# The opening of a block kernel rearranged: first input half ahead of the columns, statistics ahead of the SiLU, late zero products out, W_B's first block ahead of its shift

## The chip, the cores and the metric

The kernel runs on one core of a Trainium2 chip. The metric is device time in microseconds (us) of one execution, and the figure compared is the median over runs. A core has five instruction streams that matter here: TensorE (PE in the profile, with its weight loads as PEld), VectorE (DVE), ScalarE (ACT), GpSimd (POOL) and SyncE (SP), which in this kernel issues all the DMAs. Each engine runs its own stream strictly in order and waits on semaphores that other engines or DMAs raise.

## The reference

The input `x` has 16 sequences of 1024 positions and 256 features, all in float32. What is computed, cut to what matters:

```python
mod = (silu(c) @ wmod).reshape(16, 6, 1, -1)       # c: 16 x 256
sa, ca, ga, sb, cb, gb = (mod[:, n] for n in range(6))
ga, gb = [sign(g) * max(abs(g), 0.25) for g in (ga, gb)]
h = layernorm(x) * (1 + ca) + sa
Bu = (h @ W_B.T + b_B) * dt                        # dt = exp(log_dt)
xs[t] = A_bar * xs[t - 1] + Bu[t]                  # A_bar = exp(-exp(log_A) * dt)
x = x + ga * (xs @ W_C.T + b_C + h @ W_D.T + b_D)
h = layernorm(x) * (1 + cb) + sb
y = square(relu(h @ W_fc.T)) @ W_proj.T            # 256 -> 1024 -> 256
x = x + gb * (spikes in five steps driven by y) / 5
```

Three things in it are needed at the very start: the modulation (`silu(c)` times parts of `wmod`), the decay `A_bar`, and the statistics of the first rows of `x`.

## The kernel before

The work is cut into 32 tiles of 512 positions. A tile has two halves of work. Half "a": statistics, normalised rows `xn_a`, turned so that features lie on partitions, scaled to `h_a`, products with W_B (`pb`), a scan along positions (`xs`), products with W_D and W_C that add up in `py`, and the residual sum `x1`. Half "b": statistics of `x1`, `h_b`, the products `pf` with W_fc and `pp` with W_proj, and the spike count. Each matrix product is done in three passes on float32 operands split into a rounded high part and a remainder ("hi" and "lo"): hi by hi, weight lo by data hi, weight hi by data lo. With two blocks of 128 on the contraction that makes six TensorE products for each 128 x 512 result. The order of passes is `PASSES = ((0, 0), (1, 0), (0, 1))`, with the weight's part first (line 228).

All engine calls go through a small class that keeps each engine's instructions in the order in which the program is written (lines 71 to 83), so nothing is moved by a scheduler. Because that helper records every instruction, nearly all rows of the profile carry the same line, L81, and one goes by the names of the tiles instead.

The change touches only the opening, from the first loads to the turned rows of tile 1; the later periods, two tiles or so deep in a software pipeline, are as before. In the order in which TensorE meets it, the opening of the kernel before is:

- Loads on SP's queue (lines 125 to 152): the columns `col` (20.5 KB with c, the log of A, the biases and the log of dt), the first tile's rows `xq` in two halves of 256 KB, then parts of `wmod` (`wm1`), W_B (`fb`), W_D (`fd`), W_C (`fcm`), the second tile's rows, and more.
- `run_idle(12)` (line 612): twelve products of a tile of zeros into `ps_zero`, whose result is not used. `run_idle(3)` follows twice more (lines 616, 618).
- `silu_c` (line 182): three exponentials on ScalarE from `col`, then three VectorE steps that make `sil` = silu(c).
- `columns` (line 212) multiplies `sil` with a part of `wmod`: `ps_ca`, `ps_sa`, `ps_ga`, `ps_cb`, `ps_sb`, four small products each, which the profile shows as eight.
- `decay(n)` (line 208) issues the next n of 20 tiny VectorE steps that make `abar` (a polynomial, then squared eight times); they are strewn between other VectorE work.
- `moments`, `aggregate`, `root`, `newton_v` (lines 250 to 310): the statistics (`st_a`, `mv_a`), a square root on ScalarE (`q_a`), and five VectorE steps to the scale `r_a` and the offset `m_a`. `normalise_by` (line 324) then makes `xn_a`, four blocks of 128 x 256, each on the engine that a list names: V for VectorE, S for ScalarE.
- `transpose` turns `xn_a` into `pt_a` on TensorE; `scaled_hi` (ScalarE) and `scaled_lo` (VectorE) make `h_a`; `wb`, `wd` and `wc` are the split weights, hi on ScalarE and lo on VectorE.
- `ps_bb`, the shift `sa` times W_B, gives `bias_b`; `state_input` is `pb`; `state_bias` and `state_scan` give `bu` and `xs`; `mix_h` and `mix_xs` are `py`; `ps_ga` and `ps_bd` give the gate `ga` and its offset `gac` (`shift_gate`, line 658).
- `mix_out_late` makes `x1` (tile `x` in the profile) on ScalarE and VectorE, and `transpose_back` turns it into `pm`, from which tile 0's half "b" starts.

Of the kernel before, what the change touches and what calls it, by code (L numbers as in the profile page):

```python
# [21 lines left out]
F32 = mybir.dt.float32  # L22
# [7 lines left out]
KD = D // P  # L30
# [56 lines left out]
def adaln_kernel(ctx: ExitStack, tc: tile.TileContext, x, xq, w_bT, w_cT, w_dT, w_fcT, w_projT, cols,  # L87
# [35 lines left out]
        Q.dma_start(out=xqs[t], in_=xq[t])  # L123

    col = const.tile([P, KD * NB + 4 * KD + 1], F32, name="col")
    Q.dma_start(out=col, in_=cols)
    xqs[0] = io.tile([P, SUB, D], F32, tag="xq", name="xq_0", bufs=2)
    for s in (slice(0, 2), slice(2, 4)):
        Q.dma_start(out=xqs[0][:, s], in_=xq[0][:, s])
    cs = col[:, 0:KD * NB].rearrange("p (k b) -> p k b", k=KD)  # L130
    la, bb, bc, bd = (col[:, KD * (NB + n):KD * (NB + n + 1)] for n in range(4))
    ldt = col[:, KD * (NB + 4):]
# [49 lines left out]
    def silu_c():  # L182

        S.activation(sil, cs, AF.Exp, scale=-1.0)
        S.activation(edt, ldt, AF.Exp)
        S.activation(ea, la, AF.Exp)
        V.tensor_scalar(sil, sil, 1.0, None, ALU.add)
        V.reciprocal(sil, sil)
        V.tensor_tensor(sil, sil, cs, ALU.mult)

    def decay_steps():


        yield V.tensor_scalar(z, ea, edt, -1.0, ALU.mult, ALU.mult)
        yield V.tensor_scalar(z, z, -104.0, 1.0 / 256, ALU.max, ALU.mult)
        factor, r = 1.0, z
        for n in range(9, 1, -1):
            factor *= n
            yield V.scalar_tensor_tensor(abar, r, factor, z, ALU.add, ALU.mult)
            r = abar  # L200
        yield V.tensor_scalar(abar, abar, 1.0 / factor, None, ALU.mult)
        for _ in range(8):
            yield V.scalar_tensor_tensor(abar, abar, 2.0, abar, ALU.add, ALU.mult)
        yield V.tensor_scalar(abar, abar, 1.0, None, ALU.add)
# [3 lines left out]
    def decay(n):  # L208
        for _ in range(n):
            next(steps, None)  # L210

    def columns(wm, which, name):

        ps = ps_f.tile([P, KD, NB], F32, tag="ps_f", name=f"ps_{name}")
        for m in range(KD):
            at = which * D + m * P
            for k in range(KD):
                PE.matmul(ps[:, m], lhsT=wm[:, k, at:at + P], rhs=sil[:, k], start=k == 0, stop=k == KD - 1)
        return ps
# [27 lines left out]
    def blocks_of(x):  # L247
        return lambda s: x[:, s]

    def moments(key, src, between=lambda: None, blocks=range(SUB)):  # L250
        if key not in norms:
            n = norms[key] = Norm()
            n.sts = [small.tile([P, 6], F32, tag=f"st{s}{key[0]}", name=f"st_{key}_{s}", bufs=2)
                     for s in range(SUB)]
        for s in blocks:
            V.bn_stats(norms[key].sts[s], src(s))
            between()
# [14 lines left out]
    def root(key):  # L272
        n = norms[key]
        n.q = small.tile([P, SUB], F32, tag="q", name=f"q_{key}")
        if hasattr(n, "v"):
            S.activation(n.q, n.v, AF.Sqrt)
        else:
            S.activation(n.q, n.mv[:, :, 1], AF.Sqrt, bias=eps)
# [19 lines left out]
    def newton_v(key, between=lambda: None):  # L298

        n = norms[key]  # L300
        n.e, n.r, n.m = (small.tile([P, SUB], F32, tag=tag, name=f"{tag}_{key}") for tag in "erm")
        V.reciprocal(n.q, n.q)
        between()
        V.scalar_tensor_tensor(n.e, n.q, -0.5, n.q, ALU.mult, ALU.mult)
        between()
        V.scalar_tensor_tensor(n.e, n.mv[:, :, 1], EPS, n.e, ALU.add, ALU.mult)
        between()
        V.scalar_tensor_tensor(n.r, n.e, 1.5, n.q, ALU.add, ALU.mult)
        between()
        V.scalar_tensor_tensor(n.m, n.mv[:, :, 0], -1.0, n.r, ALU.mult, ALU.mult)  # L310
# [13 lines left out]
    def normalise_by(key, src, engines):  # L324

        n = norms.pop(key)
        xn = work.tile([P, SUB, D], F32, tag="xn", name=f"xn_{key}", bufs=3)
        for s, E in enumerate(engines):
            if E is S:
                S.activation(xn[:, s], src(s), AF.Identity, bias=n.m[:, s:s + 1], scale=n.r[:, s:s + 1])  # L330
            else:
                E.tensor_scalar(xn[:, s], src(s), n.r[:, s:s + 1], n.m[:, s:s + 1], ALU.mult, ALU.add)
        xns[key] = xn
# [37 lines left out]
        for k in range(KD):  # L371
            S.activation(hs[key][:, 0, k], src(k), AF.Identity, scale=scale[:, k])

    def scaled_lo(key, src):
        h, scale = hs[key], scale_of(key)
        for k in range(KD):
            V.scalar_tensor_tensor(h[:, 1, k], src(k), scale[:, k], h[:, 0, k].bitcast(F32),
                                   ALU.mult, ALU.subtract)

    def turned_hi(key):  # L380
        scaled_hi(key, lambda k: vs[key][:, k])
# [7 lines left out]
    def transpose(key, pool=ps_f, tag="ps_f"):  # L389

        xn = xns.pop(key)
        for k in range(KD):
            ps = pts[key, k] = pool.tile([P, TT], F32, tag=tag, name=f"pt_{key}_{k}")
            for s in range(SUB):
                dst = ps[:, s * P:(s + 1) * P]
                if key[0] == "a":
                    dst = ps.rearrange("p (q s u) -> p s q u", s=SUB, u=32)[:, s]
                PE.transpose(dst, xn[:, s, k * P:(k + 1) * P], ident)
# [11 lines left out]

    pbs = {}

    def state_input(t):
        h = hs[f"a{t}"]
        for m in range(KD):
            ps = pbs[t, m] = ps_f.tile([P, TT], F32, tag="ps_f", name=f"pb_{t}_{m}")
            products(ps, lambda i, k: wb[:, i, k, m * P:(m + 1) * P], lambda j, k: h[:, j, k], True, True, True)

# [21 lines left out]
    def state_lo(t, blocks=slice(0, KD)):  # L440
        V.tensor_tensor(xsps[t][:, 1, blocks], xss[t][:, blocks], xsps[t][:, 0, blocks].bitcast(F32),
                        ALU.subtract)

    def mix_part(t, w, v, first, last):
        for passes in (PASSES[:2], PASSES[2:]):
            for m in range(KD):
                products(ys[t, m], lambda i, k: w[:, i, k, m * P:(m + 1) * P], lambda j, k: v[:, j, k],
                         first and passes[0] == PASSES[0], last and passes[0] != PASSES[0], True, passes, True)

    def mix_h(t):  # L450
        for m in range(KD):
            ys[t, m] = ps_y.tile([P, TT], F32, tag="ps_y", name=f"py_{t}_{m}")
        mix_part(t, wd, hs[f"a{t}"], True, False)

    def mix_xs(t):
        mix_part(t, wc, xsps[t], False, True)
# [151 lines left out]
    def run_idle(n):  # L608
        for _ in range(n):
            PE.matmul(ps_zero, lhsT=zero[:, 0:P].bitcast(F32R), rhs=zero.bitcast(F32R), start=True, stop=True)  # L610

    run_idle(12)
    silu_c()
    S.activation(sa[:, 0, 0:1], edt, AF.Sqrt)
    ps_ca = columns(wm1, 1, "ca")
    run_idle(3)
    ps_sa = columns(wm1, 0, "sa")
    run_idle(3)
    decay(3)
    moments("a0", blocks_of(xqs[0]), between=lambda: decay(1))  # L620
    aggregate("a0")
    root("a0")
    S.activation(wb[:, 0], fb, AF.Identity, scale=edt)
    newton_v("a0", lambda: decay(1))
    normalise_by("a0", blocks_of(xqs[0]), (V, S, V, S))
    S.activation(sa, ps_sa, AF.Copy)
    V.tensor_scalar(s1, ps_ca, 1.0, None, ALU.add)
    V.scalar_tensor_tensor(wb[:, 1], fb, edt, wb[:, 0].bitcast(F32), ALU.mult, ALU.subtract)
    transpose("a0")
    decay(5)  # L630

    ps_bb = ps_p.tile([P, KD, NB], F32, tag="ps_p", name="ps_bb")
    for m in range(KD):
        for k in range(KD):
            PE.matmul(ps_bb[:, m], lhsT=fb[:, k, m * P:(m + 1) * P], rhs=sa[:, k],
                      start=k == 0, stop=k == KD - 1)
    scaled_hi("a0", lambda k: pts["a0", k])
    scaled_lo("a0", lambda k: pts["a0", k])
    S.activation(wd[:, 0], fd, AF.Copy)
    for m in range(KD):  # L640
        V.tensor_scalar(bias_b[:, m], ps_bb[:, m], bb[:, m:m + 1], edt, ALU.add, ALU.mult)
    decay(8)
    V.tensor_tensor(wd[:, 1], fd, wd[:, 0].bitcast(F32), ALU.subtract)
    S.activation(wc[:, 0], fcm, AF.Copy)
    state_input(0)
    state_bias(0)
    state_scan(0, (0,))
    moments("a1", blocks_of(xqs[1]), blocks=(0, 1))
    mix_h(0)

    ps_ga = columns(wm1, 2, "ga")
    ps_bd = ps_p.tile([P, KD, NB], F32, tag="ps_p", name="ps_bd")
# [13 lines left out]

    state_hi(0, slice(0, 1))
    state_scan(0, (1,))
    moments("a1", blocks_of(xqs[1]), blocks=(2, 3))
    aggregate("a1")  # L670
    root("a1")
    state_hi(0, slice(1, 2))
    V.tensor_tensor(wc[:, 1], fcm, wc[:, 0].bitcast(F32), ALU.subtract)
    state_lo(0, slice(0, 1))
    gates = shift_gate()
    newton_v("a1", lambda: next(gates, None))
    state_lo(0, slice(1, 2))
    for _ in gates:
        pass
    normalise_by("a1", blocks_of(xqs[1]), (S, S, V, S))  # L680
    mix_xs(0)
    transpose("a1")
    ps_cb = columns(wm2, 1, "cb")
    ps_sb = columns(wm2, 0, "sb")
    mix_out_late(0)
    V.tensor_scalar(s2, ps_cb, 1.0, None, ALU.add)
    scaled_hi("a1", lambda k: pts["a1", k])
# [349 lines left out]
```

## Time and profile before

| | us |
|---|---|
| median of 3 runs | 992.76 (991.89 to 993.47) |
| the profiled execution | 991.63 |
| its span, first to last instruction | 989.8 |
| TensorE busy (PE) | 981.9, 99% of the span |
| VectorE busy (DVE) | 851.1, 86% |
| ScalarE busy (ACT) | 767.1, 77% |
| GpSimd busy (POOL) | 284.5, 29% |
| granted TensorE clock, mean over the span | 0.999 |

Times in the views are counted from the span's start. A row gives start, duration, engine, operation, tiles as out<-in, how often, and in brackets how long the engine had been idle and who ended that. Ends of matrix products are modelled by the profiler, so TensorE's busy time includes short waits between products; where waits of a tenth of a microsecond matter, distances between starts are used.

### The profile page before, as it was taken

How to read it: one execution, taken by the hardware profiler on the slowest of the kernel's cores; microseconds unless marked ns; L12 is line 12 of the kernel's file. 1: busy time of each engine (PE TensorE's matmuls, PEld its weight loads, DVE VectorE, ACT ScalarE, POOL GpSimd, SP SyncE). 2: the span in 40 equal slices, each digit the busy share in tenths (PEclk: the TensorE clock that was granted, in tenths of full speed). 3: DMA queues.
4: the chain of work that ended last, by engine and by line, in shares of the span. 5: the costliest groups of instructions: out<-in, count | busy, mean ns of one | idle time of the engine just before them, and what ended most of it. 6: DMA issues, size and time to landing. Idle time of an engine off the chain costs nothing.

```text
span 989.8 us, 13366 instructions
## 1 busy us (share of the span) xinstructions
PE 981.9 (99%) x4410; PEld 813.8 (82%) x4410; DVE 851.1 (86%) x1618; ACT 767.1 (77%) x1142; POOL 284.5 (29%) x313
## 2 busy tenths in 40 slices
PE   9999999999999999999999999999999999999997
PEld 8888788888888888888888888888888888888886
DVE  8789998888988889888889888889888889887777
ACT  6786887787877887877877877877877878777784
POOL 0002243223233223233133333133332233331122
PEclk9999999999999999999999999999999999999999
DMA  8224555455454455554455454554554554443321
GB/s 312 83 82 153 179 182 149 149 171 168 153 170 137 152 179 153 157 171 133 154 179 158 155 172 127 169 170 152 168 152 146 170 167 153 149 139 128 96 86 43
DMA packets 125350, 150.07 MB, mean 152 GB/s; under 512 B 9568, under 2 KB 89184, under 8 KB 125280
## 3 DMA queue, kind: packets, MB, share of 16 engines
q1 hardware_dynamic: 125280, 149.22, 48.1%
q8 instruction: 34, 0.56, 0.2%
q14 instruction: 36, 0.29, 0.1%
HBM read 85.22 MB, written 63.96 MB: 151 GB/s over the span
## 4 chain that ended last, share of the span: by engine, by line
PE 91%; DVE 5%; ACT 2%; issue 1%; DMA 0%; SPq 0%; DVEq 0%
PE pf L81 33%; PE pp L81 32%; PE py L81 16%; PE pb L81 8%; DVE o L81 2%; PE ps_zero L81 1%; ACT a L81 1%; ACT xn_a L81 1%; ACT hid L81 0%; DMA hop_x<-w_x 0%; DVE h_b L81 0%; DVE st_b L81 0%; DVE x L81 0%; DVE h_a L81 0%; DVE e_b L81 0%
## 5 line engine op out<-in xcount | busy, mean ns | idle before, releaser
L81 PE MATMUL pp<-hid,wp 128*128 128x512 f32 (+1 forms) x1560 | 365.4, 387 | 0.4 <-DVE o L81 0.4
L81 PE MATMUL pf<-h_b,wf 128*128 128x512 f32 x1536 | 363.9, 390 | 0.0
L81 PEld LDWEIGHTS pp<-hid,wp 128*128 128x128 f32 x1560 | 289.2, 188 | 61.4 <-DVE hid L81 1.5
L81 PEld LDWEIGHTS pf<-h_b,wf 128*128 128x128 f32 x1536 | 288.1, 188 | 59.8
L81 ACT ACTIVATE a<-pf,bias_f 128x512 f32<-128x512 f32 x256 | 167.0, 680 | 157.1 <-PE pf L81 157.0
L81 DVE TENSOR_TENSOR hid<-a,hid 128x1024 fp32r<-128x1024 f32 x127 | 152.8, 1223 | 89.2 <-ACT hid L81 89.2
L81 POOL TENSOR_TENSOR o<-o,x 128x512 f32<-128x512 f32 x64 | 110.0, 1739 | 296.0 <-ACT o L81 296.0
L81 DVE SCALAR_TENSOR_TENSOR o<-pp,o 128x512 f32<-128x512 f32 (+1 forms) x260 | 177.5, 683 | 8.0
L81 ACT ACTIVATE hid<-a 128x1024 fp32r<-128x1024 f32 x128 | 135.9, 1061 | 4.0
L81 ACT ACTIVATE a<-a 128x1024 f32<-128x1024 f32 x128 | 135.8, 1061 | 3.9
L81 POOL TENSOR_SCALAR x<-x,gac 128x512 f32<-128x512 f32 x58 | 90.2, 1564 | 51.8 <-DVE o L81 51.8
L81 POOL TENSOR_SCALAR v_a<-mv_a 128x4 f32<-128x4 f32 x26 | 15.6, 600 | 278.0 <-DVE mv_a L81 278.0
L81 PE MATMUL py<-xsp,wc 128*128 128x512 f32 x384 | 92.7, 390 | 0.0
L81 PE MATMUL pb<-h_a,wb 128*128 128x512 f32 x384 | 92.6, 390 | 0.0
L81 PE MATMUL py<-h_a,wd 128*128 128x512 f32 x384 | 92.2, 389 | 0.0
L81 PEld LDWEIGHTS py<-h_a,wd 128*128 128x128 f32 x384 | 72.1, 188 | 14.9
L81 PEld LDWEIGHTS pb<-h_a,wb 128*128 128x128 f32 x384 | 71.9, 188 | 15.0
L81 PEld LDWEIGHTS py<-xsp,wc 128*128 128x128 f32 x384 | 71.8, 188 | 15.0 <-DVE xsp L81 0.3
L81 ACT ACTIVATE xn_a<-xq,m_a,r_a 128x256 f32<-128x256 f32 x123 | 63.8, 592 | 3.2 <-DVE m_a L81 3.2
L81 ACT ACTIVATE xn_b<-xm,m_b,r_b 128x256 f32<-128x256 f32 x120 | 62.0, 588 | 4.0 <-DVE m_b L81 4.0
L81 DVE TENSOR_SCALAR o<-pp 128x512 f32<-128x512 f32 (+1 forms) x65 | 43.4, 668 | 14.1 <-PE pp L81 14.1
L81 ACT ACTIVATE o<-o,gb 128x512 f32<-128x512 f32 x64 | 42.3, 709 | 6.2 <-issue 4.7
(124 smaller groups left out, 835.6 us busy)
## 6 DMA issues: line engine op xcount, KB each, us to landing
x<-in_x SPq DMA_DIRECT2D x32, 512.0 KB, 5.1
out<-o SPq DMA_DIRECT2D x63, 256.0 KB, 6.9
xq<-in_xq SPq DMA_DIRECT2D x31, 512.0 KB, 6.7
hop_a<-w_a SPq DMA_DIRECT2D x120, 128.0 KB, 2.2
v_a<-hop_a SPq DMA_DIRECT2D x30, 512.0 KB, 4.0
hop_x<-w_x SPq DMA_DIRECT2D x120, 128.0 KB, 3.1
xm<-hop_x SPq DMA_DIRECT2D x30, 512.0 KB, 3.2
hop_b<-w_b SPq DMA_DIRECT2D x120, 128.0 KB, 2.2
```

The costliest lines, as they stand in the source:

```text
L81: return self.tc.keep_in_program_order(issue(*args, **kwargs))
```

## The change

In words:

- Loads: the first half of tile 0's rows is issued ahead of `col`, which now stands between the two halves.
- `silu_c` keeps its three exponentials; its three VectorE steps become the first three steps that `decay` hands out. The statistics of tile 0 (`moments`) now begin on VectorE ahead of them, with one such step after each block. `ps_ca` comes after that in the program, and `decay(3)` goes.
- Both `run_idle(3)` go.
- `xn_a` of tile 0: VectorE, ScalarE, VectorE, VectorE in place of V, S, V, S. W_B's hi part on ScalarE moves behind its block of `xn_a`. `ps_sa` moves behind the transposes on TensorE.
- `state_input` can do one block; W_B's first block (`pb_0_0`) now comes ahead of `ps_bb`, the second one behind it.
- `mix_h` can take its passes in another order; tile 0's first `py` uses hi-hi, weight hi by data lo, weight lo by data hi. W_D's lo part moves on VectorE from ahead of the first scan to behind it.
- Tile 1's statistics, which had stood in two pairs after the two scans, move behind `xsp` lo and W_C's lo part; its `xn_a` uses S, V, S, V in place of S, S, V, S; on TensorE its transposes move behind `ps_cb` and `ps_sb`.

```diff
     col = const.tile([P, KD * NB + 4 * KD + 1], F32, name="col")
-    Q.dma_start(out=col, in_=cols)
     xqs[0] = io.tile([P, SUB, D], F32, tag="xq", name="xq_0", bufs=2)
     for s in (slice(0, 2), slice(2, 4)):
         Q.dma_start(out=xqs[0][:, s], in_=xq[0][:, s])
+        if s.start == 0:
+            Q.dma_start(out=col, in_=cols)
...
         S.activation(ea, la, AF.Exp)
-        V.tensor_scalar(sil, sil, 1.0, None, ALU.add)
-        V.reciprocal(sil, sil)
-        V.tensor_tensor(sil, sil, cs, ALU.mult)
 
     def decay_steps():
+        yield V.tensor_scalar(sil, sil, 1.0, None, ALU.add)
+        yield V.reciprocal(sil, sil)
+        yield V.tensor_tensor(sil, sil, cs, ALU.mult)
...
-    def scaled_lo(key, src):
+    def scaled_lo(key, src, between=lambda: None):
         h, scale = hs[key], scale_of(key)
         for k in range(KD):
             V.scalar_tensor_tensor(h[:, 1, k], src(k), scale[:, k], h[:, 0, k].bitcast(F32),
                                    ALU.mult, ALU.subtract)
+            between()
...
-    def state_input(t):
+    def state_input(t, blocks=range(KD)):
         h = hs[f"a{t}"]
-        for m in range(KD):
+        for m in blocks:
...
-    def mix_part(t, w, v, first, last):
-        for passes in (PASSES[:2], PASSES[2:]):
+    def mix_part(t, w, v, first, last, order=PASSES):
+        for passes in (order[:2], order[2:]):
...
-    def mix_h(t):
+    def mix_h(t, order=PASSES):
...
-        mix_part(t, wd, hs[f"a{t}"], True, False)
+        mix_part(t, wd, hs[f"a{t}"], True, False, order)
...
     run_idle(12)
     silu_c()
     S.activation(sa[:, 0, 0:1], edt, AF.Sqrt)
+    moments("a0", blocks_of(xqs[0]), between=lambda: decay(1))
     ps_ca = columns(wm1, 1, "ca")
-    run_idle(3)
-    ps_sa = columns(wm1, 0, "sa")
-    run_idle(3)
-    decay(3)
-    moments("a0", blocks_of(xqs[0]), between=lambda: decay(1))
     aggregate("a0")
     root("a0")
+    newton_v("a0", lambda: decay(1))
+    normalise_by("a0", blocks_of(xqs[0]), (V, S, V, V))
     S.activation(wb[:, 0], fb, AF.Identity, scale=edt)
-    newton_v("a0", lambda: decay(1))
-    normalise_by("a0", blocks_of(xqs[0]), (V, S, V, S))
+    V.tensor_scalar(s1, ps_ca, 1.0, None, ALU.add)
+    decay(2)
+    V.scalar_tensor_tensor(wb[:, 1], fb, edt, wb[:, 0].bitcast(F32), ALU.mult, ALU.subtract)
+    decay(1)
+    transpose("a0")
+    ps_sa = columns(wm1, 0, "sa")
+    scaled_hi("a0", lambda k: pts["a0", k])
+    scaled_lo("a0", lambda k: pts["a0", k], lambda: decay(1))
     S.activation(sa, ps_sa, AF.Copy)
-    V.tensor_scalar(s1, ps_ca, 1.0, None, ALU.add)
-    V.scalar_tensor_tensor(wb[:, 1], fb, edt, wb[:, 0].bitcast(F32), ALU.mult, ALU.subtract)
-    transpose("a0")
-    decay(5)
+    decay(6)
+    S.activation(wd[:, 0], fd, AF.Copy)
+    S.activation(wc[:, 0], fcm, AF.Copy)
+    state_input(0, (0,))
 
     ps_bb = ps_p.tile([P, KD, NB], F32, tag="ps_p", name="ps_bb")
...
-    scaled_hi("a0", lambda k: pts["a0", k])
-    scaled_lo("a0", lambda k: pts["a0", k])
-    S.activation(wd[:, 0], fd, AF.Copy)
+    state_input(0, (1,))
     for m in range(KD):
         V.tensor_scalar(bias_b[:, m], ps_bb[:, m], bb[:, m:m + 1], edt, ALU.add, ALU.mult)
     decay(8)
-    V.tensor_tensor(wd[:, 1], fd, wd[:, 0].bitcast(F32), ALU.subtract)
-    S.activation(wc[:, 0], fcm, AF.Copy)
-    state_input(0)
     state_bias(0)
     state_scan(0, (0,))
-    moments("a1", blocks_of(xqs[1]), blocks=(0, 1))
-    mix_h(0)
+    V.tensor_tensor(wd[:, 1], fd, wd[:, 0].bitcast(F32), ALU.subtract)
+    mix_h(0, (PASSES[0], PASSES[2], PASSES[1]))
...
     state_hi(0, slice(0, 1))
     state_scan(0, (1,))
-    moments("a1", blocks_of(xqs[1]), blocks=(2, 3))
+    state_hi(0, slice(1, 2))
+    state_lo(0, slice(0, 1))
+    V.tensor_tensor(wc[:, 1], fcm, wc[:, 0].bitcast(F32), ALU.subtract)
+    state_lo(0, slice(1, 2))
+    moments("a1", blocks_of(xqs[1]))
     aggregate("a1")
     root("a1")
-    state_hi(0, slice(1, 2))
-    V.tensor_tensor(wc[:, 1], fcm, wc[:, 0].bitcast(F32), ALU.subtract)
-    state_lo(0, slice(0, 1))
     gates = shift_gate()
     newton_v("a1", lambda: next(gates, None))
-    state_lo(0, slice(1, 2))
     for _ in gates:
         pass
-    normalise_by("a1", blocks_of(xqs[1]), (S, S, V, S))
+    normalise_by("a1", blocks_of(xqs[1]), (S, V, S, V))
     mix_xs(0)
-    transpose("a1")
     ps_cb = columns(wm2, 1, "cb")
     ps_sb = columns(wm2, 0, "sb")
+    transpose("a1")
     mix_out_late(0)
```

## The prediction, made before the changed kernel had run

> **What bounds the kernel now.** I read the page first, then the chain of work that ended last in order of time, then the timeline of each engine over the first 32 us, and last the loads. The page's busy times:
>
> ```profile
> PE 981.9 (99%) x4410; PEld 813.8 (82%) x4410; DVE 851.1 (86%) x1618; ACT 767.1 (77%) x1142; POOL 284.5 (29%) x313
> ```
>
> TensorE is the bound. Busy time includes modelled ends, so I also looked at the distances between starts of products: from 6 us on, hardly one is over 0.1 us above the pace (0.228 us for a 512-column product, as in the twelve of `py` in 2.72 us). So the kernel's time is the length of TensorE's own list, and the change can gain only what it takes out of that list, less what waits come in. The chain in order of time (start, length, what) shows the list where the change works:
>
> ```profile
> 1.47 4.47 PE ps_zero L81 x12
> 5.93 0.92 PE ps_ca L81 x8
> 6.85 0.79 PE ps_zero L81 x3
> 7.64 0.80 PE ps_sa L81 x8
> 8.44 0.80 PE ps_zero L81 x3
> 9.24 0.87 PE pt_a L81 x8
> ...
> 21.22 0.87 PE pt_a L81 x8
> 22.09 0.80 PE ps_cb L81 x8
> 22.89 0.89 PE ps_sb L81 x8
> 23.78 0.92 PE pm L81 x8
> 24.70 2.77 PE pb L81 x12
> ```
>
> The reader is to see two rows of three zero products, 0.79 and 0.80 us, and that everything else is needed. Who feeds TensorE stands in the timeline (start, length):
>
> ```profile
> 6.01 0.30 ACT L81 ACTIVATE q_a<-mv_a,edt 128x4 f32<-128x4 f32 x1 [1.57 <-DVE mv_a L81]
> ...
> 7.34 1.09 ACT L81 ACTIVATE xn_a<-xq,m_a,r_a 128x256 f32<-128x256 f32 x2 [0.27 <-DVE m_a L81]
> 7.34 0.73 DVE L81 TENSOR_SCALAR xn_a<-xq,r_a,m_a 128x256 f32<-128x256 f32 x2
> ...
> 20.44 0.19 DVE L81 TENSOR_TENSOR gac<-gac,ga 128x32 f32<-128x32 f32 x1
> ...
> 21.12 1.42 ACT L81 ACTIVATE x<-py,gac,ga 128x512 f32<-128x512 f32 x2
> ...
> 21.92 1.36 DVE L81 TENSOR_TENSOR x<-x,x 128x512 f32<-128x512 f32 x2 [0.96 <-ACT x L81]
> ```
>
> Tile 0's `xn_a` is done at 8.43, so the first transposes could start 0.7 us before they do: the last zero products cover that. And `x1` is added by 23.28, just ahead of `pm` at 23.6: the second feeder is exactly in time, with no slack to give. That row decides my forecast.
>
> **The change, part by part.**
>
> *Taken off TensorE's list:* six zero products, 0.79 + 0.80 = 1.59 us. This is the most that can be gained; it is 0.16% of the time, and about 0.2% (2.0 us) is what a measurement of this kernel can tell from no change.
>
> *The loads.* The issues and landings are these (size, median us from issue to landing):
>
> ```profile
> xq<-in_xq SPq DMA_DIRECT2D x2, 256.0 KB, 2.8
> col<-in_cols SPq DMA_DIRECT2D x1, 20.5 KB, 1.8
> ```
>
> The first half goes from 1.15 to 0.72 and so lands at about 3.4 instead of 3.8. `col` is issued at 1.15 and lands between 2.95 (1.8 later) and 3.5 (behind the 256 KB ahead of it); I take 3.45, since both use one queue, against 2.5 before. The second half landed at 4.5; 4.3 to 4.5 now. The loads behind them keep their places.
>
> *Statistics of tile 0.* On VectorE the four blocks stood at 4.02, 4.42, 4.81 and 5.21. Now the first stands at 3.4, but the three SiLU steps (0.18, 0.35, 0.19) lie between, and the reciprocal hides only in part: the last block is at 4.9, the aggregates end at 5.77. ScalarE has the exponentials from 3.48, the table load of 1.28 us, and is free at 5.3, half a microsecond before it is needed. `q_a` is at 5.8 instead of 6.01: 0.2 gained. `ps_ca` starts at 5.8 after the twelve zero products as before, since `sil` is ready at 5.0.
>
> *xn_a and the transposes.* From `q_a` to `xn_a` it took 7.34 - 6.01 = 1.33 us; so 7.13. Three blocks on VectorE at distances of 0.33 end at 8.2. TensorE is through with `ps_ca` at 6.85 and now waits: first block at 7.54, first transpose at 7.6, fourth block 8.2, last transpose ends at 8.8. Dense it would be 6.85 + 0.87 = 7.72, so 1.1 of the 1.59 us turn into waiting. W_B's hi part (0.72) fits on ScalarE between 7.63 and 8.36, `h_a` hi follows at 8.58 (9.71 before), W_B's lo at 8.45 to 9.19 on VectorE.
>
> *To the first py.* `ps_sa` covers 8.8 to 9.7, by then the hi parts are there (9.26 and 9.84). Then `pb_0_0` (six products, 1.37), `ps_bb` (0.8 to 0.9), `pb_0_1` (1.37), and one more change from small to large products (0.09): `py` starts at about 13.35 instead of 13.66. Net so far: 0.3 gained.
>
> *What is late next.* `bias_b` waits for `ps_bb`, which is now behind six large products: 12.15 instead of 11.76, +0.39. Behind it on VectorE is one unbroken train, 9.2 us long (11.76 to 20.96), and all of it moves. W_D's lo part, now behind the first scan, ends at 15.16; TensorE wants it at 13.35 + 8 x 0.228 = 15.17: a wait of 0 to 0.1. The scans' hi and lo parts come earlier than before (the last lo at 18.07 instead of 20.20), but `py` from W_C wanted them at 18.0 to 19.9 anyway: no gain. Tile 1's statistics come last. Their square root on ScalarE (0.30 plus two hand-overs, 0.36) was hidden behind W_C's lo part and a state's lo part, and now VectorE stands still for it. Two waits for just-written results (0.15 together) come with the new order. So the gate `gac` ends at 20.63 + 0.39 + 0.36 + 0.15 = 21.53, and `m_a` at 21.1 instead of 19.6.
>
> *The turned tile 1.* `ps_cb` and `ps_sb` ahead of the transposes cover this: TensorE reaches the transposes at 22.5, and `xn_a` (two blocks each from 21.13 and 21.45) ends at 22.2. No wait.
>
> *x1.* ScalarE makes two blocks of `xn_a` (1.0 us) before `x1`: 22.13 instead of 21.12. VectorE adds at 22.92 and 23.59, ending 23.61 and 24.28. TensorE, dense, comes to `pm` at 23.4: it waits 0.27 for the first four transposes and 0.2 for the second four. Tile 1's `pb` starts at 24.85 instead of 24.46.
>
> *From there.* Tile 0's second statistics on VectorE are 1.0 later (25.6 instead of 24.6), `xn_b` ends at 30.3 instead of 29.7; TensorE wants its last block at 30.43 + 0.33. Covered, with 0.4 to spare; without that cover each 0.1 is 0.1 on the end. Behind that, no row shows TensorE waiting, and I count nothing.
>
> The sum: -1.59 (zero products) + 1.1 (waiting for `xn_a`) + 0.1 (more changes of size) + 0.1 (W_D's lo) + 0.7 (`x1`, which comes late against a TensorE that was 0.3 ahead) = +0.4 us. On the profiled execution, 989.8 + 1.83 around the span = 991.63, this gives 992.0; the median of the runs is 1.13 above the profiled one, so 993.2.
>
> *The clock at the start.* One row speaks for a little less. The windows over `ps_zero` (stretch, us, PE busy and count, PEld, PEclk, DMA, GB/s):
>
> ```profile
> 1.46:4.60 3.14, 3.13 (x7) 2.48 (x8) 1.00 0.71 237
> 4.60:6.00 1.40, 1.33 (x6) 0.75 (x4) 1.00 1.02 323
> ```
>
> Seven zero products in 3.14 us are 0.43 each, about twice the 0.228 of the later ones, although the column says 1.00: TensorE ran at half pace until 4.6. Where that lasts longer in another run, the kernel before pays at once, half of each added microsecond; the changed one has 0.77 us of waiting before its first transpose to absorb it. If the 1.13 us between profile and median are of this kind, some 0.4 to 0.8 of them go. I take 0.4 off: 992.8.
>
> [...]
>
> **The rivals.**
>
> *Gain kept.* If `x1` were not late, the 0.3 gained at `py` would stay, and with a long half-pace start up to 1.1: 991.7 to 992.5. Against it: the add of `x` ended 0.3 us before `pm` and everything ahead of it moves by 0.9. Even all 1.59 is not 0.2%.
>
> *The clock falls back (slower).* Between 6.85 and 9.7 TensorE has only transposes, tiny products and waits, and from 20.7 to 24.8 again. Price: the start shows 3.1 us at half pace; the same over dense products loses half, 1.5 us, and twice that if it happens at both places: 994.3 to 995.8. It decides once the granted clock is below 1.00 for some 3 us. Against it: 21.22 to 24.70 was as thin, 3.48 us without a large product, at 1.00; the new stretch is 4.1.
>
> *VectorE becomes the bound.* If each new hand-over costs 0.1 more, the train brings `x1` and then `xn_b` 0.5 to 1.2 us later still: 993.3 to 994.0.
>
> *The load brings nothing.* If `col` lands at 4.0, behind more than I assume, the SiLU holds the statistics and `q_a` comes at 6.2: 0.4 later on the whole train, 993.2.
>
> **How the numbers follow.** Forecast 0.56, gain kept 0.08, clock 0.10, VectorE 0.14, load 0.12. Slower by over 0.2% is most of the clock case and the tail of VectorE's: 0.12. Faster by over 0.2% needs the gain kept and more than I can name: 0.04. The rest, 0.84, is within. The range takes in the gain-kept end (991.7) and the VectorE end (994.0) with 0.5 for the wait sizes that no row shows: 991.7 to 994.5.
>
> **What would show it.** Right: `q_a` near 5.8; TensorE without `ps_zero` after 6 and with a gap before `pt_a`; `bias_b` near 12.2; `gac` near 21.5; `pm` waiting for DVE `x`; tile 1's `pb` near 24.85; the rest unchanged. Wrong: half pace after 5 us; `pt_b` waiting for `xn_b`; or new waits of TensorE after 32 us.

## The result, and the profile after

| | before | after |
|---|---|---|
| median of 20 runs, us | 992.58 (991.75 to 993.47) | 995.50 (992.84 to 998.80) |
| ratio of the medians | | 1.0029, 95% interval 1.0021 to 1.0037 |
| the profiled execution, us | 991.63 | 992.84 |
| its span, us | 989.8 | 991.1 |
| mean granted clock of the runs | 0.999 (of the profiled one) | 0.992 to 0.999 |

The change costs 2.9 us. The prediction was 992.8 with a range to 994.5; the median lies above that range, on the side that it gave 0.12. The profiled execution of the changed kernel happens to be the shortest of its 20, and the table's last row says what the others have: six runs with a mean clock of 0.998 or 0.999 lie between 992.84 and 993.73 us (median 992.94), and the fourteen with 0.992 to 0.997 between 994.37 and 998.80. By and large, the lower a run's mean clock, the longer its time (0.998 at 992.84, 0.995 at 995.23 to 996.45, 0.992 at 998.80). So the page and the timeline below show the change without its main cost, which makes them a good place to read the prediction's steps one by one.

From the page, the busy times:

```profile
PE 981.5 (99%) x4404; PEld 813.3 (82%) x4404; DVE 852.2 (86%) x1620; ACT 766.1 (77%) x1140; POOL 284.5 (29%) x313
```

Six products fewer on TensorE, and still a span 1.3 us longer. The timeline (start, length, in brackets the idle time ahead) has the rows that answer to those shown of before:

```profile
6.00 0.30 ACT L81 ACTIVATE q_a<-mv_a,edt 128x4 f32<-128x4 f32 x1 [0.54 <-DVE mv_a L81]
...
7.33 1.06 DVE L81 TENSOR_SCALAR xn_a<-xq,r_a,m_a 128x256 f32<-128x256 f32 x3
...
7.89 1.32 PE L81 MATMUL pt_a<-ident,xn_a 128*128 128x128 f32 x8 [1.03 <-DVE xn_a L81]
...
12.40 0.50 DVE L81 TENSOR_SCALAR bias_b<-ps_bb,col,edt 128x16 f32<-128x16 f32 x2
...
21.75 0.19 DVE L81 TENSOR_TENSOR gac<-gac,ga 128x32 f32<-128x32 f32 x1
...
22.54 1.42 ACT L81 ACTIVATE x<-py,gac,ga 128x512 f32<-128x512 f32 x2
...
23.33 1.36 DVE L81 TENSOR_TENSOR x<-x,x 128x512 f32<-128x512 f32 x2 [0.74 <-ACT x L81]
...
24.08 1.32 PE L81 MATMUL pm<-ident,x 128*128 128x128 f32 x8 [0.20 <-DVE x L81]
...
25.16 2.99 PE L81 MATMUL pb<-h_a,wb 128*128 128x512 f32 x12
```

The reader is to see three things. `q_a` is where it was (6.00, before 6.01), so the earlier load and the earlier statistics brought nothing; `xn_a` starts at 7.33, before 7.34. TensorE stands still 1.03 us ahead of `pt_a`, where zero products had stood. And `x` is added by 24.69 instead of 23.28, `pm` waits for it, and tile 1's `pb` starts at 25.16 instead of 24.46. The loads (size, median us from issue to landing):

```profile
xq<-in_xq SPq DMA_DIRECT2D x2, 256.0 KB, 2.8
...
col<-in_cols SPq DMA_DIRECT2D x1, 20.5 KB, 2.3
```

`col` takes 2.3 us instead of 1.8, and lands at 3.5 as predicted. In the prediction's first windows the clock column said 1.00 while the pace was half. The trace also holds the moments at which the granted clock changes, and those are used from here on: TensorE starts at half pace (zero products start 0.43 us apart), is granted full speed at 4.88 in this execution (0.23 us apart from there on), and keeps it to 987.92; its last product ends at 984.62. In the trace of the kernel before full speed is granted from 4.60 to 987.64. Both stretches are 983.04 us long, 288 times 3.4133.

### The profile page after: what moved, and what is told of

It reads as the page before. It is cut to its first block, busy times and chain, and to the rows that moved or that the text cites. A ratio compares the mean times of both kernels' runs of the same rounds, so it can differ in the third digit from the quotient of the medians.

```text
span 991.1 us, 13352 instructions
## 1 busy us (share of the span) xinstructions
PE 981.5 (99%) x4404; PEld 813.3 (82%) x4404; DVE 852.2 (86%) x1620; ACT 766.1 (77%) x1140; POOL 284.5 (29%) x313
## 4 chain that ended last, share of the span: by engine, by line
PE 83%; DVE 6%; issue 5%; ACT 3%; DMA 1%; POOL 1%; SPq 0%; DVEq 0%; ACTq 0%; POOLq 0%
PE pf L81 30%; PE pp L81 30%; PE py L81 15%; PE pb L81 8%; DVE o L81 2%; ACT a L81 1%; POOL o L81 1%; ACT xn_a L81 1%; DVE xs L81 0%; DMA hop_b<-w_b 0%; DMA v_b<-hop_b 0%; DVE xsp L81 0%; ACT hid L81 0%; DVE st_a L81 0%; DVE x L81 0%
```

## The experiments

Three theories. **A**: somewhere in the first 12 us there is now a stretch in which TensorE has too little to do, and the granted clock falls back to half there, in most runs. **B**: the same, but in the second thin stretch at 21 to 25 us, where `pm` now waits. **C**: no clock; late data (the loads, the VectorE train) makes the time. Each run gives a median with the kernel before run beside it on the same chip, and a ratio with its 95% interval; the ratio is the one on record and can differ from the quotient of the two medians by up to 0.0007.

### The changed kernel again

Nothing in it is changed.

> The changed kernel once more. Theory A (the granted clock falls back because of the first thin stretch of TensorE, 5.9 to 9.9 us, with its gap of 1.0 us) and theory B (it falls back because of the second thin stretch, 20.9 to 25.2 us) both expect runs that differ by up to 6 us, the longer ones with a lower mean granted clock (0.992 to 0.997 against 0.999), and in the trace of a longer run a stretch of products at twice the distance of 0.228 us: by A it begins between 8 and 14 us, by B between 21 and 29 us. Theory C (the clock has no part in it, the longer runs come from the data chain or the loads) expects products at 0.228 throughout and gaps ahead of them.

997.78 us median (5 runs), before 993.05: ratio 1.0047 [1.0035, 1.0059]. This time the profile fell on a run with a mean clock of 0.993. Its windows (stretch, us, then PE busy with the number of products, PEld, DVE, ACT, POOL, granted clock at the end of the row, DMA share, GB/s):

```profile
3.09:6.50 3.41, 3.41 (x10) 2.47 (x8) 2.13 (x9) 1.90 (x5) 0.00 (x0) 1.00 0.82 262
6.50:9.91 3.41, 2.47 (x19) 1.98 (x18) 2.98 (x21) 1.76 (x4) 0.00 (x0) 1.00 1.01 358
9.91:13.32 3.41, 3.41 (x15) 3.02 (x14) 2.98 (x12) 2.25 (x5) 0.00 (x0) 0.50 1.02 417
13.32:16.74 3.42, 3.42 (x14) 3.03 (x13) 0.76 (x5) 0.50 (x1) 0.00 (x0) 0.50 1.03 422
16.74:20.15 3.41, 3.41 (x10) 2.64 (x9) 2.88 (x5) 1.40 (x3) 0.00 (x0) 0.50 1.03 398
20.15:23.56 3.41, 3.41 (x24) 3.06 (x22) 3.41 (x8) 0.63 (x1) 0.00 (x0) 1.00 0.44 152
```

The bounds of the rows are not chosen for neatness: the clock is released at 6.50, taken back at 9.91 and released again at 20.15, and each distance is a whole number of 3.413 us (one at full speed, three at half). Afterwards 285 of these stretches pass at full speed. (Ahead of the first release the column reads 1.00 as well, though ten products in 3.41 us are half pace.) So in this trace, as in the first one and in before's, the changes of the clock lie a whole number of 3.413 us apart. A window, from here on, is a stretch of that length counted from a change. The one ahead of the loss is 6.50 to 9.91: from `ps_ca` to `ps_sa`, with the gap in it. Theory A, and not at B's place. The size fits as well: 10.24 us at half speed lose half of that, 5.1 us, and this execution is 4.7 above the median of before beside it.

### The gap filled

```diff
     ps_ca = columns(wm1, 1, "ca")
+    run_idle(3)
     aggregate("a0")
```

> The changed kernel with three zero products put behind the first columns product, where TensorE waits for 1.0 us anyway: 0.7 us of work in that gap. Theory A expects the spread to go: all runs between 992.5 and 993.8, mean clock 0.998 or 0.999, ratio to before about 1.0005. Theory B expects the spread to stay, 993 to 999 with a median near 995.5. Theory C expects no change, or 0.1 us more.

994.44 us (11 runs, 0.997 to 0.999), ratio 1.0013 [1.0004, 1.0022]; the clock did not fall in the trace. Three products whose result nobody uses take 3.3 us off the changed kernel's median. Theory A had expected all runs below 993.8, and that did not come: they go up to 995.32. Of the 1.4 us that are left, a part may still be the clock, since the three longest runs (994.86 to 995.32) have a mean clock of 0.997; but the eight at 0.998 and 0.999 have a median of 994.01, 1.0 over before, and there the clock is not the reason.

### The kernel before without its late zero products

```diff
     ps_ca = columns(wm1, 1, "ca")
-    run_idle(3)
     ps_sa = columns(wm1, 0, "sa")
-    run_idle(3)
     decay(3)
```

> The kernel before with nothing changed but the two groups of three zero products taken out. Theory A expects this alone to bring the spread: runs from 991 to 998 and mean clocks down to 0.993, since TensorE then has only small products and a wait from 5.9 to 8.5 us. Theory B expects no spread, since the second stretch is as in the kernel before: 991.5 to 992.6, ratio 0.999 to 1.000. Theory C expects the same as B.

994.78 us (11 runs), ratio 1.0013 [1.0003, 1.0023]; eight of the eleven at a mean clock of 0.997 or less. So one part of the change, alone and with the old order of everything else, already lets the clock fall, in most runs. In its trace it is taken back after this window:

```profile
6.26:9.68 3.42, 3.16 (x25) 2.66 (x24) 2.95 (x18) 2.31 (x6) 0.00 (x0) 1.00 1.04 364
```

TensorE is busy 3.16 of 3.42 us here, and the window before's 4.60 to 8.01 has 3.41. The window that loses its clock is nearly full of work by the busy column. What the work is differs much more: one large product begins in it, the other 23 stream 128 columns or 16.

### Tile 1 as before, without and with the gap filled

The changed kernel with the part behind the shift (W_D's lo part, the passes of the first `py`, tile 1's statistics, `xn_a` and transposes) put back as in the kernel before; the second one with `run_idle(3)` behind `ps_ca` as well.

> The changed kernel with all that concerns tile 1 and W_D's lo part as in the kernel before; the loads, the SiLU, the missing zero products and W_B's first block ahead of its shift stay changed. Theory A expects the spread to stay (mean clocks down to 0.993, median near 995), with the shortest runs 0.3 to 0.6 us below the shortest of the changed kernel. Theory B expects it to go: median 992.0 to 992.8. Theory C expects a median 0.3 to 0.6 us below that of the changed kernel and a spread like it.

> Tile 1's part and W_D's lo part as in the kernel before, and three zero products in the gap behind the first columns product. With theory A (a window of 3.41 us with few streamed columns makes the clock fall; below about 2000 it fell, from 2430 up it held) the spread goes, as it nearly did with the three zero products alone, and what is left over there (1.1 us above before) goes with tile 1's part, if the late x1 makes it: median 992.6 to 993.4 against 993.05 of before. If the 1.1 us came from later loads or a longer half-pace start instead, it stays: 993.9 to 994.6.

Without the fill 996.65 us (11 runs, nine at 0.997 or less), ratio 1.0034 [1.0024, 1.0044], though `pm` no longer waits: theory B falls, since the second stretch is as it was. With the fill 994.11 us (11 runs, 0.997 to 0.999), ratio 1.0017 [1.0008, 1.0026]: what is left over before does not go with tile 1's part, as the first case of its expectation had it. Nor is the shortest run without the fill (993.17) below the changed kernel's shortest (992.84), as A had expected. The profile of the first fell on a run that kept its clock.

### The gap filled with thin products, and with twice as many large ones

```diff
     ps_ca = columns(wm1, 1, "ca")
+    for _ in range(4):
+        PE.matmul(ps_zero[:, 0:NB], lhsT=zero[:, 0:P], rhs=zero[:, 0:NB], start=True, stop=True)
     aggregate("a0")
```

> The changed kernel with the gap behind the first columns product filled by four float32 products of 16 columns in place of three of 512: as much time (0.9 us), hardly any columns (the profile counts eight passes, 128 columns together). If idle time of TensorE makes the clock fall, this cures it like the three zero products: runs 993 to 995, mean clock 0.998 to 0.999. If the columns streamed in a window make it fall, it cures nothing: runs up to 998, mean clocks down to 0.993, median 995 to 997.

> Three zero products in the gap and three more behind the transposes: as many as in the kernel before. Theory A expects no run with a mean clock below 0.998, thus a spread of 2 us at most, but 0.6 to 0.8 us more in every run than the shortest with three, since the second group stands on TensorE's path: 993.8 to 995.5. If the spread comes from elsewhere, it stays.

The thin products fill time with 16 columns each: 996.90 us (5 runs, all at 0.992 to 0.995), ratio 1.0047 [1.0035, 1.006], nothing cured. In the trace the clock falls after this window and stays at half for four windows:

```profile
5.02:8.43 3.41, 2.27 (x16) 1.78 (x14) 2.37 (x18) 1.07 (x4) 0.00 (x0) 1.00 1.03 345
```

This one window is no test of busy time, since `ps_ca` waited 1.1 us for its load in it and only three of the eight thin products began in it; the medians are. With three large products in the gap and three behind the transposes: 994.67 us (11 runs, 0.997 to 0.999), ratio 1.0015 [1.0004, 1.0025]; the second three bring nothing more, and two runs at 0.997 show that the spread is not quite gone. So it matters what fills the gap: with three large products there (0.79 us in the kernel before) the runs have a mean clock of 0.997 to 0.999, with the thin ones (eight records of 16 columns in a row, as in `ps_sa`, take 0.80 us) 0.992 to 0.995.

### The loads

The filled kernel with `col` loaded first as before; the kernel before, unchanged; and the kernel before with only the loads exchanged.

> The changed kernel with three zero products in the gap, and the columns loaded first as in the kernel before. The SiLU steps still stand between the statistics. If the first half ahead of the columns gains anything, this one is 0.2 to 0.4 us slower than with the changed loads (994.6 to 994.8 against 994.4); if the loads bring nothing, it is the same within 0.2.

> The kernel before once more, for its own spread and a second trace. Theory A (few streamed columns in a window of 3.41 us make the clock fall; it fell at 2224 and below, held at 2432 and above) expects the clock held, since the first trace had at least 3072 columns in every window after the release: 992 to 993.8, mean clock 0.998 to 0.999. If the loads land later here (the first columns part of the modulation at 6.5 to 7.2 us instead of 5.7), TensorE's list from there on is 0.5 to 1.3 us later, with no wait behind it.

> The kernel before with the first input half loaded ahead of the columns, nothing else. The SiLU is then 1.0 us later, at 4.6 us, still ahead of the load that its first product waits for (5.7 us or later), and the statistics start 0.4 us earlier at the most, under the cover of the zero products: no change expected, ratio 0.9995 to 1.0005, clock held. If the order of loads alone lets the later loads land later (as in the runs with it, 6.6 to 7.1 us), 0.3 to 0.8 us slower.

Filled with the old loads: 993.60 us (11 runs), ratio 1.0009 [1.0, 1.0018]. Before again: 993.00 us, 0.9995 [0.9986, 1.0004]. Before with the new loads: 993.24 us (12 runs), 1.0004 [0.9995, 1.0014]; three of its runs have a mean clock of 0.994 to 0.997, where it had been expected to hold, but so have five of the 35 of before beside it. The exchange alone is worth nothing that can be measured. With the fill it is 994.44 against 993.60, the old loads 0.8 us shorter, which neither case had expected; these are two medians from different chips, and the intervals of their ratios overlap.

### Half of the zero products, and the first part of the change alone

The kernel before without its second `run_idle(3)`; and the changed kernel with the gap filled and loads and tile 1 as before, so that only the earlier statistics, the later shift and W_B's first block remain.

> The kernel before without the second group of three zero products, the first group kept. TensorE is then 0.8 us earlier at the transposes and waits 0.1 to 0.3 us for the normalised rows: 0.4 to 0.6 us gained, if the clock holds. By theory A it holds: the thinnest window of 3.41 us (three zero products, eight transposes, small ones) has 2600 to 2900 columns. Then 992.3 to 992.6, ratio 0.9994 to 0.9997. If any zero product that goes lets the clock fall, runs above 995 with clocks of 0.995 and less, as without both groups.

> The changed kernel with three zero products in the gap, with the loads and tile 1's part as in the kernel before: what remains is the statistics ahead of the SiLU, the columns' shift behind the transposes and W_B's first block ahead of the shift. If tile 1's part makes the base of 0.9 to 1.3 us over before, this is at 992.8 to 993.2 (ratio 1.000). If W_B's first block ahead of the shift makes it (the bias on VectorE 0.6 to 1.6 us later, and the whole train behind it), it stays at 993.6 to 994.1 (1.0007 to 1.0012).

One row less: 992.17 us (12 runs, 991.42 to 996.34), the lowest median of all, ratio 0.9991 [0.9979, 1.0004]. Ten runs lie at 991.42 to 992.44, two at 995.75 and 996.34 with a mean clock of 0.996. The ten lie some 0.8 us below before; by the interval the kernel is not shown to be faster, and two runs of twelve with a lower clock, against five of 35 of before beside it, do not show that it risks more. The first part alone: 993.66 us (11 runs), ratio 1.0003 [0.9994, 1.0012]. By its median this is the second case of the expectation (`bias_b` starts at 12.73 in its trace, before at 11.76), but the interval leaves the first one open, and in the trace `ps_ca` also waited 0.63 us for its load.

### The tile 1 part alone, and the shift ahead again

The kernel before with the tile 1 part of the change; and the kernel of the last experiment with `ps_bb` back ahead of both blocks of `pb`.

> The kernel before with the tile 1 part of the change alone: tile 1's statistics in one piece behind the second scan, its transposes behind ps_cb and ps_sb, its xn_a on S, V, S, V, W_D's lo part behind the first scan with the passes of the first py turned. Loads, statistics of tile 0, both rows of three zero products and the shift stay as before. If the tile 1 part makes the missing 0.3 us (x1 late by what the prediction reckoned, 0.36 + 0.15 + two blocks of xn_a on ScalarE, against bias_b at its old 11.8): gac comes about 0.5 later than in the kernel before (20.9 to 21.0), pm waits 0.3 or more for DVE x, tile 1's pb starts 0.3 to 0.5 later than before, 24.8 to 25.3, and the time is 0.3 to 0.5 us over the kernel before, with the clock kept (mean 0.997 to 0.999). If the lateness of bias_b is what makes x1 late, pm waits 0.1 or less here, and tile 1's pb starts within 0.1 of the kernel before.

> The kernel with only the first part of the change (statistics ahead of the SiLU, shift product behind the transposes, three zero products kept behind ps_ca, loads and tile 1 as before), with ps_bb back ahead of both blocks of pb. If bias_b behind six large products is the mis-sized term: bias_b starts near 11.4 instead of 12.7, TensorE waits 0.1 to 0.4 us for sa in front of ps_bb, gac comes 0.8 or more earlier than the 21.41 of the kernel with W_B's block first, and tile 1's pb starts 0.3 to 0.6 earlier than 25.43 there. If the order of ps_bb and pb costs nothing, tile 1's pb starts at the same place to within 0.15, whatever gac does.

The first: 992.72 us against 992.45 (11 and 23 runs), ratio 1.0004 [0.9995, 1.0012], one run at a mean clock of 0.996, the others at 0.998 or more. From its timeline:

```profile
21.75 0.19 DVE L81 TENSOR_TENSOR gac<-gac,ga 128x32 f32<-128x32 f32 x1
...
23.33 1.36 DVE L81 TENSOR_TENSOR x<-x,x 128x512 f32<-128x512 f32 x2 [0.74 <-ACT x L81]
...
24.08 1.32 PE L81 MATMUL pm<-ident,x 128*128 128x128 f32 x8
...
25.16 3.01 PE L81 MATMUL pb<-h_a,wb 128*128 128x512 f32 x12
```

These are the changed kernel's starts to the hundredth, with both rows of zero products in place. VectorE begins its first scan at 13.65 here (13.66 in the changed kernel), and from there to `gac` it takes 8.10 us in both, against 7.00 in the kernel before (13.44 to 20.44): W_D's lo part behind the scan (0.6), the wait for the square root (0.36) and hand-overs. So what makes `x1` late behind the scan is the tile 1 part. Ahead of the scan each has a reason of its own: here VectorE waits 0.30 us for `bu`, in the changed kernel `bias_b` comes late. Against a trace of the kernel before whose clock was released at nearly the same time (5.78, here 5.86), `gac` is 0.91 late (21.75 against 20.84; 0.5 had been expected) and tile 1's `pb` 0.29 (25.16 against 24.87). The medians differ by 0.27, but their interval takes in no difference at all.

The second: 993.26 us (12 runs), ratio 1.001 [1.0, 1.002]. What it was meant to measure did not show, because in its profiled run the clock fell (`bias_b` at 13.04, expected 11.4; tile 1's `pb` at 27.29); what the order of `ps_bb` and `pb` costs by itself stays open. But it is the clearest fall of all. Two windows, and the products of the first one by tile (us busy, mean ns, idle before):

```profile
8.66:12.08 3.42, 2.99 (x24) 2.73 (x24) 3.32 (x12) 3.13 (x7) 0.00 (x0) 1.00 1.05 408
12.08:15.49 3.41, 3.41 (x10) 2.74 (x10) 2.44 (x13) 0.48 (x2) 0.00 (x0) 0.50 1.04 423
```

```profile
L81 PE MATMUL pt_a<-ident,xn_a 128*128 128x128 f32 x8 | 1.3, 289 | 0.3 <-DVE xn_a L81 0.3
L81 PE MATMUL ps_bb<-sa,fb 128*128 128x16 f32 x8 | 1.1, 273 | 0.3 <-ACT sa L81 0.3
L81 PE MATMUL ps_sa<-sil,wm 128*128 128x16 f32 x8 | 1.0, 252 | 0.0
```

Twenty-four products, no idle time over 0.35 us, 2.99 of 3.42 us busy, and the clock is taken back at the end of the window. Three zero products fill the gap in this kernel too, but they start at 7.47, ahead of the window, and it lost the clock all the same. One window later, in which eight large products began, it is there again (15.49). It cost the twelve products of `pb` 4.37 us (12.19 to 16.56) instead of 2.90 in the kernel before.

### What the windows have in common

Counting the columns that the products begun in a window stream (512, 128 or 16 each) sorts the windows of the first 30 us that begin at full speed, in the traces taken. These are the four that lost the clock, three of the thinnest that kept it, and the kernel before's thinnest:

| kernel, window | products of 512, 128, 16 columns | columns | clock after it |
|---|---|---|---|
| changed, again, 6.50 to 9.91 | 0, 8, 9 | 1168 | half, 3 windows |
| shift ahead again, 8.66 to 12.08 | 0, 8, 16 | 1280 | half, 1 window |
| before without zero products, 6.26 to 9.68 | 1, 7, 16 | 1664 | half, 2 windows |
| thin products, 5.02 to 8.43 | 4, 0, 11 | 2224 | half, 4 windows |
| tile 1 as before, 21.43 to 24.85 | 2, 9, 16 | 2432 | full |
| changed, first profile, 4.88 to 8.29 | 4, 3, 8 | 2560 | full |
| filled, old loads, 6.51 to 9.92 | 3, 7, 8 | 2560 | full |
| before, 21.66 to 25.08 | 3, 10, 16 | 3072 | full |

A window of large products alone has 15 of them, 7680 columns (252 of the 288 at full speed in the trace of before). Neither busy time nor the number of products, nor that of the large ones alone, sorts these windows: the one of the changed kernel's first profile kept the clock with fewer products and less busy time than three of the four that lost it, and 2 large products kept it where 4 had not.

```profile
4.88:8.29 3.41, 2.38 (x16) 2.07 (x15) 3.01 (x20) 1.82 (x5) 0.00 (x0) 1.00 1.04 355
```

At half clock the count sorts less well. The changed kernel run again had 2672 and 2176 columns in its windows from 9.91 and 13.32, TensorE busy all the time, and the clock was not released. It was released behind 2624 columns at the start of the filled kernel with tile 1 as before; behind seven large products (3584 columns) at 4.60 in the kernel before; and behind eight (4096) at 4.88 in the changed kernel's first profile, at 20.15 where it was run again, and at 15.49 in the kernel with the shift ahead again. At the end of the kernel, where TensorE's work runs out, the traces of the kernel before and of the changed kernel kept full speed through 5888 and 7168 columns (980.81 to 984.22 and 981.09 to 984.50) and lost it after a window in which no product began.

## Why the prediction was wrong

**The step that failed** is "The clock at the start", and with it the chance of 0.10 for "The clock falls back". The prediction took 0.4 us off because the changed kernel "has 0.77 us of waiting before its first transpose to absorb" a longer half pace. In its sum the six zero products stand at -1.59 us, and for the clock at nothing. The runs show the opposite: with the zero products gone, that stretch is where the clock is lost, for 10.24 us in the traced run. Fourteen of the twenty runs have a lower mean clock, and the median is 2.6 us above that of the six that kept it (995.50 against 992.94). Nor does the waiting make a late release harmless: of the two traces of the changed kernel, the one released later (6.50 against 4.88) lost its clock. The release stands on the same steps of 3.413 us as the loss. At 4.88 the next window still takes in four of the twelve zero products (2560 columns, kept); at 6.50 it begins where they end (1168, lost).

**The argument against the rival** was the row from 21.22 to 24.70, "as thin, 3.48 us without a large product, at 1.00". It was not as thin. It has sixteen transposes, and the window that held most of it counts 3072 columns, 1536 of them in three large products at its edge. The new stretch has eight transposes and sixteen products of 16 columns, 1280 columns in all. Judged by the absence of large products the two are alike, counted in columns they are not. Both counts could have been made from the trace of before and the order of the new products, though nothing in that trace said that columns were what to compare.

**The rival's price** was right: 994.3 to 995.8 was forecast for it, and the median is 995.50. Its working was not: one place and not two, and three windows at half pace there, in the traced run, and not one. That the price fits is luck.

**The base** was +0.4 us on the profiled execution and came out at +1.2 (992.84 against 991.63), +0.7 of it by tile 1's `pb`. The lateness stays at 0.6 to 0.7 us through the middle of the kernel; the rest comes in the last period and behind the last product (the last `pf` starts 0.86 late, the span is 1.3 longer). Such waits differ from trace to trace: the second trace of the kernel before starts its first `pf` 0.41 later than the first trace and its last one 1.03 later. The six runs that kept their clock have a median 0.36 over before's (992.94 against 992.58), which is the size of the prediction's sum and close to its 992.8; for the runs that kept their clock the base was sized about right. By its steps:

- `q_a` at 5.8: it was 6.00. The third block of statistics waited for the second half of `xq`, which landed at 4.67 (5.54 where the changed kernel was run again); 4.3 to 4.5 had been taken. So `pt_a` came 0.3 late (7.89), and the 0.3 us gained at `py` is gone (13.68 for 13.35).
- `bias_b` at 12.15: 12.40, 0.25 late for the same reason, and the VectorE train with it.
- W_D's lo part, a wait of 0 to 0.1: 0.28 us of idle time of the weight load.
- `gac` done at 21.53: 21.94, and `x1` done at 24.69 for 24.28, 0.41 late both. Of that 0.25 is `bias_b`; 0.16 is the train, from `bias_b` to `gac` 9.35 us instead of 8.68 + 0.51. W_D's lo part had stood between the last step of `abar` and the first scan. It started 0.08 us after that step; the scan, which needs its result, starts 0.27 after it. No row of before showed that hand-over, because the part that moved had hidden it.
- `pm` waiting 0.27 and 0.2: the weight loads of its two halves wait 0.43 and 0.25, the products of the first half 0.20.
- The mechanism of that step stands: `x1` is late against a TensorE with nothing in hand, and takes back what the zero products had given.

**Right** were the bound, the terms of the sum in their signs, and that `pt_b` does not wait for `xn_b`. "VectorE becomes the bound" did not happen beyond `x1`, and "The load brings nothing" did in its outcome, `q_a` is where it was, though not by its mechanism: `col` landed at 3.5, and the second half of the rows was late.

**Open:** where a limit lies, if there is one (in the opening 2224 columns lost the clock and 2432 kept it), and whether columns are what decides or only what goes with it. Why the filled kernels stay 0.6 to 1.7 us over before, though the clock was kept in all their traces (late release, 6.51 with the old loads against 4.60 in the kernel before, late loads and later waits are in them, in no fixed shares). And why a few runs of the kernel before also show a lower mean clock (5 of 35 in one set, 994.4 to 997.1 us): none of them was traced.

## What to carry to other kernels

Before taking work off TensorE, count the columns that it streams in each 3.4 us around the place (the step of the granted clock in these traces), for every position that such a window could have, and compare with the thinnest window that has kept its clock (here 2432 columns; 2224 lost it); busy time and the number of products did not sort the windows here. Products whose result nobody uses were what held the clock here: three large ones in the gap gave 994.44 us where the changed kernel without them had 997.78, so filling a gap with such products is a cheap test of it. And read the mean granted clock of every run beside its time: one profile, here the luckiest of twenty, can show a kernel without its main cost.

## What the runs showed of the hardware

- In the traces of the kernel before and of the changed kernel, the granted clock stood at full speed for 983.04 us (from 4.60 and 4.88 us on), 288 times 3.4133. Where the changed kernel was run again, it was released at 6.50, taken back at 9.91 and released at 20.15, one and three times 3.413 us apart.
- Windows that were busy for most of their length lost the clock: 2.99 us busy of 3.42 (1280 columns, shift ahead again), 3.16 of 3.42 (1664 columns, before without zero products). Float32 products of 16 columns, with records of 0.25 to 0.28 us each and 0.8 us for eight in a row, did not hold it: four more of them in the gap left the median at 996.90 us and the mean clocks at 0.992 to 0.995.
- After a loss, half speed went on for one window (shift ahead again), two (before without zero products), three (the changed kernel again) and four (thin products, 8.43 to 22.08). In the windows behind a loss that did not end it, TensorE was busy all the time; in the changed kernel again they had 2672 and 2176 columns.
- The same 256 KB, issued at 1.63 and 1.62 in two profiles of the changed kernel, landed at 4.67 and at 5.54.
